# A graph layer on one core: row gathers listed behind the evictions of picked rows, each waiting for its eviction, where they were listed with the use of chunks

## The chip, the core and the metric

The kernel runs on one core of one Trainium2 chip. The metric is device time in microseconds (us), from the launch's start to its end. Times of the kernel before: 2096.8, 2087.51 and 2089.18 us, median 2089.18. A kernel's program keeps five queues of instructions: TensorE (PE, with its weight loads as PEld), VectorE (DVE), ScalarE (ACT), GpSimd (POOL) and SyncE (SP). Each queue runs in order, and semaphores tie the queues together.

## The reference

A graph layer with two kinds of edges, a residual connection and a layer norm. There are 12,500 nodes of 128 features and 400,000 edges, sorted by destination.

```python
Xs = X[src]
m_data = Xs @ W_data.T + b_data
m_ctrl = Xs @ W_control.T + b_control
msg = where(edge_types == 0, m_data, m_ctrl)
agg = segment_sum(msg, dst, num_segments=12500)
out = relu(agg + X @ W_self.T + b_self)
result = layernorm(X + out)
```

The kernel sums the source rows first and multiplies by the weights afterwards: for each node it needs the sum of the rows that come by edges of type 0, the sum of those of type 1, and how many there were of each (for the biases).

## The kernel before

**Chunks and groups.** The edges are cut into 3125 chunks of 128. 125 chunks make a group, 25 groups in all. A group has five windows of 5 "p" chunks and 20 "e" chunks; in odd groups the fifth window is 25 "p" chunks. That makes 865 p chunks, and 113 windows of e chunks, one after the other: the main loop's 113 steps (`for w in range(pairs)`, near the end of `short_path`).

**x in three parts.** Ahead of the loop, x is split into three bf16 parts whose sum is the f32 value. They stay in SBUF (`x3`) and are also written to DRAM as rows of 384 bf16 numbers (`rows3`).

**p chunks are gathered.** `fetch` (L721) takes a buffer `msg` from a pool of HOLD = 18 and lets GpSimd fetch 128 rows of `rows3` by an indirect DMA (L727). AHEAD = 14 of them are issued ahead of the loop. After that, `chunk` (L741) calls `fetch` once as it uses a chunk, so that the gather listed with chunk n is that of chunk n + 14. It can start once its buffer is free, which is when the matmuls of the chunk 18 before its own are done. Using a chunk takes three matmuls with a 0/1 matrix of destinations (`add_rows`, L677) and one that counts (L753); they add up in a PSUM tile `sums`, which VectorE adds to an accumulator (L715) when the window is done.

**e chunks are picked.** The rows of an e window are put into 98 blocks of 32 slots by the block of x that they come from. For each block TensorE multiplies a 0/1 matrix (`pick`) with that block of x in SBUF (L782), so that the wanted rows land in PSUM (`got`), four blocks in 128 rows. ScalarE evicts them to bf16 as `emsg`, two such sets at a time (L793, "the eviction of picked rows", 12 a step). TensorE then counts (L804) and adds them up (L677) as it does p chunks. Edges that don't fit in 32 slots, up to 64 a step, are fetched by one more indirect DMA of GpSimd into a tile `last` (`spare_rows`, L761); its index comes from VectorE (`idx`, L519). The other half of `last` is the two remaining blocks, evicted by L799.

**VectorE's part.** For each step VectorE works out which block and slot each edge gets, in a chain of bf16 operations: `O`, `prod`, `half`, `found`, `rm`, `rv` (L482 to L608). TensorE puts `rv` in place (`rk`, L620), ScalarE copies it (`cell`), and two DMAs of SyncE spread it over all partitions as the next steps' `pick` (L630, L632).

**What sets the order.** The kernel lists its work by fractions of a step: `evenly` gives units a place between 0 and 1, and `merged` (L142) sorts several streams by place and traces them in that order. The p chunks are spread evenly over all steps (`chunks`), at place `at` = LAG + (n + 0.5) (pairs - LAG) / total for the n-th. A step of `picked` (L766) is six units; unit t holds two evictions (`rows`, L787), and `spare_rows` is called in unit 2. A framework makes the engines' queues and the semaphores from the traced order; the changed program leaves the order on TensorE, VectorE, ScalarE and SyncE as it is. Each gather also waits for the landing of the one eight before it.

Of the kernel before, what the change touches and what calls it, by code (L numbers as in the profile page):

```python
# [9 lines left out]
BF = mybir.dt.bfloat16  # L10
# [7 lines left out]
P = 128  # L18
D = 128
# [4 lines left out]
NG = NC // GC  # L24
GN = P * GC * N // E
PB = 5
# [3 lines left out]
NE = 5  # L30
# [13 lines left out]
NCELL = 4 * NQ  # L44
OVF = 64
TOP = 7
SB = 1
HOLD = 18
AHEAD = 14
ACC_ROWS = 99 * P  # L50
# [97 lines left out]
def evenly(units, a=0.0, b=1.0):  # L148
    return [(a + (b - a) * (k + 0.5) / len(units), u) for k, u in enumerate(units)]


def short_path(ctx, tc, const, ident, eps, wT, brow, bad, x, src, dst, etype, ws, bs, out):
    nc = tc.nc
# [19 lines left out]
    def of_p(g, i):  # L173

        return PL if g % 2 and i == NE - 1 else PB
# [46 lines left out]
    for kind, i, c, _ in windows(0):  # L222
        if kind == "p":
            n = PL if i == NE - 1 else PB
            nc.sync.dma_start(
                out=near_i[i * PB:i * PB + n, :],
                in_=dst.rearrange("(o g e) -> o g e", o=1, g=NG)[:, :, c * P].to_broadcast([n, NG]),
# [6 lines left out]
    rows3 = dram.tile([N, 3 * D], BF, name="rows3")  # L234
# [181 lines left out]
    codes = {}  # L416
# [61 lines left out]
    def select(sel, col, code2):  # L478

        rows, n, width = sel.shape  # L480
        shape = [rows, n, width // 2, 2]
        nc.vector.tensor_tensor(  # L482
            sel.rearrange("p n (w t) -> p n w t", t=2),
            col[:rows].rearrange("p (o w t) -> p o w t", o=1, t=2).to_broadcast(shape),
            code2.rearrange("p n (o t) -> p n o t", o=1).to_broadcast(shape),
            op=OP.is_equal,
        )
        return sel
# [180 lines left out]
    def sums():  # L669
        return ps2.tile([P, 512], FP, name="sums")  # L670

    def cells_of(ps, width, k):
        return ps[:, k * 2 * width:(k + 1) * 2 * width]

    def add_rows(out, msg, sel, start, stop):
        for j in range(3):
            nc.tensor.matmul(  # L677
                out, msg[:, j * D:(j + 1) * D], sel, start=(start and j == 0), stop=stop, skip_group_check=True
            )
# [28 lines left out]
    def accumulate(g, i, ps, wide, width):  # L708

        begin_acc(g)  # L710
        parts_in[g] = parts_in.get(g, 0) + 1
        with tc.issue_after(added[-2].ins) if len(added) > 1 else ExitStack():
            at = nc.vector.value_load(raw["place"][0:1, g, i:i + 1], min_val=0, max_val=R - WMAX)
        win = acc[g][:, :, bass.ds(at, width)]
        added.append(nc.vector.tensor_add(win, win, ps[:, :4 * wide].rearrange("p (a w) -> p a w", w=wide)[:, :, :width]))  # L715


    to_fetch = [(g, i, c) for g in range(NG) for i in range(NE) for c in range(0, of_p(g, i), SB)]
    fetched = []

    def fetch():  # L721
        if to_fetch:
            g, i, c = to_fetch.pop(0)
            msg = mp.tile([P, SB, 3 * D], BF, name="msg")
            for k in range(min(SB, of_p(g, i) - c)):
                at = i * PB + c + k
                nc.gpsimd.indirect_dma_start(  # L727
                    out=msg[:, k, :], out_offset=None, in_=rows3[:, :],
                    in_offset=bass.IndirectOffsetOnAxis(ap=codes["p", g][0][:, at:at + 1], axis=0),
                )  # L730
            fetched.append(msg)

    def gathered(g, i):
        n = of_p(g, i)
        s = {}

        def choose():
            sel = sp.tile([P, PL, 2 * PW], BF, name="psel")[:, :n]
            s["sel"] = select(sel, near_col, codes["p", g][1][:, i * PB:i * PB + n])

        def chunk(c):  # L741
            if c % SB == 0:
                fetch()
                s["msg"] = fetched.pop(0)
            if c == 0:
                s["ps"] = sums()
                choose()
            sel = s["sel"][:, c].rearrange("p (t w) -> p t w", t=2)
            rows, cnt = (
                cells_of(s["ps"], AW, k).rearrange("p (t w) -> p t w", t=2)[:, :, DPC * c:DPC * c + PW] for k in range(2)  # L750
            )
            add_rows(rows, s["msg"][:, c % SB, :], sel, c == 0, c == n - 1)
            nc.tensor.matmul(cnt, one_col, sel, start=False, stop=(c == n - 1), skip_group_check=True)  # L753
            if c == n - 1:
                accumulate(g, 2 * i, s["ps"], AW, PW + DPC * (n - 1))

        return evenly([lambda c=c: chunk(c) for c in range(n)])

    def spare_rows(w):
        msg = slots[w]["last"] = two.tile([P, 3 * D], BF, name="last")  # L760
        nc.gpsimd.indirect_dma_start(  # L761
            out=msg[:OVF, :], out_offset=None, in_=rows3[:, :],
            in_offset=bass.IndirectOffsetOnAxis(ap=slots[w]["idx"], axis=0),
        )

    def picked(w, tiled, ending, fin_used, before):  # L766

        g, i = each_e[w]  # L770
        s = {"sel": {}, "msg": {}}
        per, pair = 4, 2

        def choose(q0, n=8):

            sel = select(sp.tile([P, 9, 2 * EW], BF, name="esel")[:, :n], code_col, slots[w]["code"][:, q0:q0 + n])
            for k in range(n):
                s["sel"][q0 + k] = sel[:, k]

        def pick(ps, q, a0=0):  # L780
            for a in range(a0, 4):
                nc.tensor.matmul(  # L782
                    ps[CAP * a:CAP * (a + 1), :], slots[w]["pick"][:, a * NQ + q, :],
                    x3[:, 4 * q + a - a0].rearrange("p j d -> p (j d)"), start=True, stop=True, skip_group_check=True,
                )

        def rows(q):  # L787
            ps = psg.tile([P, pair, 512], FP, name="got")
            msg = two.tile([P, pair, 3 * D], BF, name="emsg", bufs=5)
            for k in range(pair):  # L790
                pick(ps[:, k, :3 * D], q + k)
                s["msg"][q + k] = msg[:, k, :]
            nc.scalar.copy(msg, ps[:, :, :3 * D])  # L793

        def last_rows():
            q = NQ - 1
            ps = psg.tile([P, pair, 512], FP, name="got")[:, 0] if fin_used else ps1.tile([P, 512], FP, name="fin")
            pick(ps[:, :3 * D], q, 2)
            nc.scalar.copy(s["msg"][q][OVF:, :], ps[OVF:, :3 * D])  # L799

        def count(q):
            if q == 0:
                s["ps"] = sums()
            nc.tensor.matmul(  # L804
                cells_of(s["ps"], EW, 1)[CAP * (q % 4):CAP * (q % 4 + 1), :], one_col[:, :CAP], s["sel"][q],
                start=(q < 4), stop=(q + 4 >= NQ), skip_group_check=True,
            )

        def add(q0, q1):
            for q in range(q0, q1):  # L810
                add_rows(cells_of(s["ps"], EW, 0), s["msg"].pop(q), s["sel"][q], False, q == NQ - 1)

        def unit(t):

            for q in range(t * per, (t + 1) * per, pair):
                rows(q)
            if t == 1 and before:
                before()
            if t in (0, 1):
                choose(8 * t)  # L820
            if t == 0:
                ending()
            if t == 2:
                if w > 0:
                    spare_rows(w)
                s["msg"][NQ - 1] = slots[w]["last"]
            if t == 3:
                choose(16, 9)
            if t > 0:
                for q in range((t - 1) * per, t * per if t < turns - 1 else NQ):  # L830
                    count(q)
            if t == turns - 1:
                last_rows()
            if t > 0:
                add((t - 1) * per, t * per)
            for u in tiled.get(t, []):
                u()

        def end():

            add((turns - 1) * per, NQ)
            for u in tiled.get(turns, []):
                u()
            accumulate(g, 2 * i + 1, s["ps"], EW, EW)

        turns = (NQ - 1) // per
        return evenly([lambda t=t: unit(t) for t in range(turns)]), end


# [111 lines left out]
    mp = ctx.enter_context(tc.tile_pool(name="msg", bufs=HOLD))  # L961
# [9 lines left out]
    load(1, "p")  # L971
    for u in prep_p(0):
        u()
    for _ in range(AHEAD):
        fetch()


    chunks, closed, rest = {}, {}, []
# [1 line left out]
    n = 0  # L980
    for p in range(NG * NE):
        for _, u in gathered(*divmod(p, NE)):
            at = LAG + (n + 0.5) * (pairs - LAG) / total
            chunks.setdefault(int(at), []).append((at % 1, u))
            n += 1
        closed.setdefault(int(at), []).append(p)

    def ending():
        pass

    for w in range(pairs):
        g, i = each_e[w]
# [197 lines left out]
```

## Time and profile before

| what | us |
|---|---|
| median of the timed runs | 2089.18 |
| the profiled execution's own time | 2084.42 |
| its span, from first to last instruction | 2082.7 |
| TensorE busy between 110 and 2060 us | 1792.47 of 1950 |
| GpSimd's gathers busy, L727 | 1153.9, in 865 of 1334 ns on average |
| the same gathers, shortest, median, longest | 0.940, 1.058, 4.247 |
| one eviction L793, median | 0.798 |

The page's lines by groups give a line of the kernel, its engine and operation, what it writes and reads, the count, the busy time and the mean length of one, and after the last bar the time that its engine stood idle ahead of it and what ended that. "issue" is time in which an engine waited for nothing that the profile shows. The trace's first 110 us are the start-up (loads, the split of x, the first picks and gathers). The mean granted clock of TensorE is 0.986.

### The profile page before, as it was taken

The numbers are of one execution on the slowest core, as the hardware profiler recorded it, in microseconds if no ns is written. First come the engines' busy times: TensorE is split into PE (matmuls) and PEld (weight loads), VectorE is DVE, ScalarE is ACT, GpSimd is POOL, SyncE is SP. The second block draws the span as 40 slices with busy tenths as digits, with TensorE's granted clock in tenths as the row PEclk, the third lists the DMA queues.
The fourth block names the chain that finished last, engine by engine and source line by source line (L and its number), as shares of the span: only waits on it lengthen the run. The fifth ranks groups of instructions, "written<-read, shape, count | busy, mean of one in ns | idle before, by whom it ended". The sixth has DMA issues, their size and how long they took to land.

```text
span 2082.7 us, 75459 instructions
## 1 busy us (share of the span) xinstructions
PE 1828.3 (88%) x30869; PEld 1369.9 (66%) x30869; DVE 1718.1 (82%) x4707; ACT 1304.3 (63%) x2464; POOL 1296.7 (62%) x996
## 2 busy tenths in 40 slices
PE   0489889999999998899998999999999999999996
PEld 0367666676666776676666666766776676776675
DVE  7689788988887888888888888878888888888873
ACT  3466666666665666666566666656666666766665
POOL 0446567667667667567666566676676676665660
PEclk9999999999999999999999999999999999999998
DMA  7534343443443443433433434434434434434331
GB/s 213 185 107 134 107 136 102 139 136 98 135 136 97 135 131 102 133 121 112 126 105 118 130 101 134 133 101 134 133 97 132 136 99 132 134 107 132 122 98 33
DMA packets 186535, 254.92 MB, mean 122 GB/s; under 512 B 85369, under 2 KB 152995, under 8 KB 183108
## 3 DMA queue, kind: packets, MB, share of 16 engines
q1 hardware_dynamic: 128418, 152.97, 22.7%
q0 software_dynamic: 45136, 90.65, 15.5%
q10 hardware_dynamic: 12626, 6.40, 1.1%
q8 instruction: 243, 3.98, 0.8%
q14 instruction: 112, 0.92, 0.1%
HBM read 231.89 MB, written 18.04 MB: 120 GB/s over the span
## 4 chain that ended last, share of the span: by engine, by line
PE 56%; DVE 30%; ACT 5%; issue 4%; DMA 2%; another core or an unknown queue 1%; DVEq 1%; SPq 0%; ACTq 0%
PE sums L677 24%; PE got L782 18%; ACT emsg L793 4%; DVE esel L482 4%; PE rk L620 3%; DVE pick L662 3%; DVE prod L570 3%; DVE rv L608 3%; PE sums L804 2%; DVE found L579 2%; DVE prod L548 2%; DVE ahead L566 2%; PE rk L556 2%; PE rk L508 1%; DVE half L575 1%
## 5 line engine op out<-in xcount | busy, mean ns | idle before, releaser
L727 POOL DMA_INDIRECT msg<-rows,pidx x865 | 1153.9, 1334 | 619.9 <-PE sums L677 251.9
L793 ACT CAST emsg<-got 128x768 bf16<-128x768 f32 x1356 | 1035.6, 802 | 494.2 <-PE got L782 371.4
L677 PE MATMUL sums<-esel,emsg 128*128 128x176 bf16 x8136 | 755.5, 241 | 11.4 <-issue 10.8
L782 PE MATMUL got<-x,pick 128*32 128x384 bf16 x10896 | 664.7, 332 | 91.8 <-ACT emsg L793 60.8
L677 PEld LDWEIGHTS <-emsg 128*128 128x128 bf16 x8136 | 598.1, 98 | 169.0 <-issue 152.5
L782 PEld LDWEIGHTS <-pick 128*32 128x32 bf16 x11074 | 260.8, 95 | 255.3 <-issue 156.0
L482 DVE TENSOR_TENSOR esel<-code_col,code 128x1408 bf16<-128x1408 bf16 x339 | 308.9, 911 | 29.0 <-PE sums L677 13.6
L715 DVE TENSOR_TENSOR acc<-acc,sums 128x352 f32 (+2 forms) x238 | 102.0, 429 | 169.2 <-PE sums L677 79.7
L761 POOL DMA_INDIRECT last<-rows,idx x113 | 138.7, 1227 | 132.8 <-DMA bias<-b_parts 71.3
L677 PE MATMUL sums<-psel,msg 128*128 128x48 bf16 x2595 | 186.0, 184 | 12.2 <-DVE acc L715 7.8
L804 PE MATMUL sums<-esel,one_col 128*32 128x176 bf16 x2825 | 183.5, 242 | 9.0 <-issue 8.4
L677 PEld LDWEIGHTS <-msg 128*128 128x128 bf16 x2595 | 149.1, 97 | 21.0 <-issue 18.1
L620 PE MATMUL rk<-rv,O 128*128 128x64 bf16 x2260 | 90.5, 195 | 68.0 <-DVE rv L608 63.8
L662 DVE TENSOR_SCALAR pick<-pick,lane_f 128x1600 bf16<-128x1600 bf16 x226 | 142.8, 637 | 6.8 <-DMA pick<-there 4.2
L482 DVE TENSOR_TENSOR O<-cell_col,blk 128x2000 bf16<-128x2000 bf16 x113 | 134.7, 1192 | 15.1 <-PE fin L782 6.3
L753 PE MATMUL sums<-psel,one_col 128*128 128x48 bf16 x865 | 145.3, 183 | 0.2 <-issue 0.2
L620 PEld LDWEIGHTS <-O 128*128 128x128 bf16 x2260 | 83.2, 100 | 93.9 <-issue 92.9
L570 DVE TENSOR_TENSOR prod<-O,ahead 128x2000 bf16<-128x2000 bf16 x113 | 134.4, 1190 | 0.0
L804 PEld LDWEIGHTS <-one_col 128*32 128x32 bf16 x2825 | 86.6, 96 | 45.8 <-issue 16.7
L566 DVE TENSOR_REDUCE ahead<-rk 128x100 bf16<-128x500 f32 x113 | 76.2, 675 | 48.6 <-PE rk L498 21.3
L753 PEld LDWEIGHTS <-one_col 128*128 128x128 bf16 x865 | 82.7, 96 | 1.2 <-issue 1.1
L579 DVE TENSOR_REDUCE found<-half 128x20 f32<-128x520 bf16 x113 | 77.4, 685 | 0.0
(173 smaller groups left out, 2026.6 us busy)
## 6 DMA issues: line engine op xcount, KB each, us to landing
pick<-there SPq DMA_DIRECT2D x113, 800.0 KB
acc<-acc_start SPq DMA_DIRECT2D x23, 1280.0 KB
msg<-rows,pidx POOLq DMA_INDIRECT x865
rows<-x SPq DMA_DIRECT2D x6, 1344.0 KB
xs<-in_x_dram SPq DMA_DIRECT2D x99, 62.5 KB
out_dram<-h SPq DMA_DIRECT2D x99, 62.5 KB
xt<-in_x_dram ACTq DMA_DIRECT2D x6, 896.0 KB
there<-cell SPq DMA_DIRECT2D x113, 6.2 KB
```

The source lines that it names most:

```text
L482: nc.vector.tensor_tensor(sel.rearrange("p n (w t) -> p n w t", t=2), col[:rows].rearrange("p (o w t) -> p o w t", o=1, t=2).to_broadcast( ...
L570: nc.vector.tensor_tensor(prod, s["O"], ahead.rearrange("p (o j) -> p o j", o=1).to_broadcast([P, EC, NCELL]), op=OP.mult)
L579: nc.vector.tensor_reduce(found, half[:, :, :26], AX.X, OP.add)
L620: nc.tensor.matmul(s["rk"][:m, :2 * CAP], s["held"][:, c * NCELL:c * NCELL + m], s["rv"][:, c].rearrange("p v r -> p (v r)"), start=(c == ...
L662: nc.vector.tensor_scalar(t, t, lane_f, None, op0=OP.is_equal)
L677: nc.tensor.matmul(out, msg[:, j * D:(j + 1) * D], sel, start=(start and j == 0), stop=stop, skip_group_check=True)
L727: nc.gpsimd.indirect_dma_start(out=msg[:, k, :], out_offset=None, in_=rows3[:, :], in_offset=bass.IndirectOffsetOnAxis(ap=codes["p", g][0] ...
L753: nc.tensor.matmul(cnt, one_col, sel, start=False, stop=(c == n - 1), skip_group_check=True)
L761: nc.gpsimd.indirect_dma_start(out=msg[:OVF, :], out_offset=None, in_=rows3[:, :], in_offset=bass.IndirectOffsetOnAxis(ap=slots[w]["idx"], ...
L782: nc.tensor.matmul(ps[CAP * a:CAP * (a + 1), :], slots[w]["pick"][:, a * NQ + q, :], x3[:, 4 * q + a - a0].rearrange("p j d -> p (j d)"), ...
L793: nc.scalar.copy(msg, ps[:, :, :3 * D])
L804: nc.tensor.matmul(cells_of(s["ps"], EW, 1)[CAP * (q % 4):CAP * (q % 4 + 1), :], one_col[:, :CAP], s["sel"][q], start=(q < 4), stop=(q + 4 ...
```

## The change

Gathers are no longer listed by `chunk`. A list `due` holds, for each gather, the place at which the chunk 14 before its own is used, and 0 for the first 14, which are still issued ahead of the loop. After each eviction of picked rows, `paced` is called with the place of that eviction. If a gather of spare rows is on the list `spare`, it is issued; else, if the next gather's due place is reached, that one is; else none. So at most one gather stands behind each eviction. `tc.add_manual_dep(..., Sync, DATA)` makes the gather wait on a semaphore until that eviction is done. The gather of spare rows moves from unit 2 to the first eviction of unit 1. The constant SB, which was 1, is gone, and with it the loop over SB.

```diff
-    to_fetch = [(g, i, c) for g in range(NG) for i in range(NE) for c in range(0, of_p(g, i), SB)]
-    fetched = []
+    to_fetch = [(g, i, c) for g in range(NG) for i in range(NE) for c in range(of_p(g, i))]
+    fetched, due, spare = [], [], []
...
+    def paced(now, gate):
+
+        if spare:
+            gather = spare.pop()()
+        elif to_fetch and due[len(due) - len(to_fetch)] <= now:
+            gather = fetch()
+        else:
+            return
+        tc.add_manual_dep(
+            gather.ins, gate.ins.name,
+            mybir.DependencyInfo(mybir.DependencyClass.Sync, mybir.DependencyReason.DATA), reason="paced",
+        )
...
         def chunk(c):
-            if c % SB == 0:
-                fetch()
-                s["msg"] = fetched.pop(0)
+            s["msg"] = fetched.pop(0)
...
-            nc.scalar.copy(msg, ps[:, :, :3 * D])
+            paced(w + (q + 1) / (turns * per), nc.scalar.copy(msg, ps[:, :, :3 * D]))
...
+            if t == 1 and w > 0:
+                spare.append(lambda: spare_rows(w))
...
             if t == 2:
-                if w > 0:
-                    spare_rows(w)
+                assert not spare
...
+            due.append(at)
             n += 1
...
+    due[:] = [0.0] * AHEAD + due[:-AHEAD]
+    for _ in range(AHEAD):
+        fetch()
```

More of the change, by code (lines that the diff above doesn't have):

```diff
@@ L46 @@
 TOP = 7
-SB = 1
 HOLD = 18
@@ L715, in accumulate @@
         added.append(nc.vector.tensor_add(win, win, ps[:, :4 * wide].rearrange("p (a w) -> p a w", w=wide)[:, :, :width]))
-    to_fetch = [(g, i, c) for g in range(NG) for i in range(NE) for c in range(0, of_p(g, i), SB)]
-    fetched = []
+    to_fetch = [(g, i, c) for g in range(NG) for i in range(NE) for c in range(of_p(g, i))]
+    fetched, due, spare = [], [], []
     def fetch():
[L722 to L731, printed above, removed]
+        g, i, c = to_fetch.pop(0)
+        msg = mp.tile([P, 3 * D], BF, name="msg")
+        at = i * PB + c
+        fetched.append(msg)
+        return nc.gpsimd.indirect_dma_start(
+            out=msg, out_offset=None, in_=rows3[:, :],
+            in_offset=bass.IndirectOffsetOnAxis(ap=codes["p", g][0][:, at:at + 1], axis=0),
+        )
[9 more added lines that the diff above has]
+            mybir.DependencyInfo(mybir.DependencyClass.Sync, mybir.DependencyReason.DATA), reason="paced",
+        )
     def gathered(g, i):
@@ L751, in chunk @@
             )
-            add_rows(rows, s["msg"][:, c % SB, :], sel, c == 0, c == n - 1)
+            add_rows(rows, s["msg"], sel, c == 0, c == n - 1)
             nc.tensor.matmul(cnt, one_col, sel, start=False, stop=(c == n - 1), skip_group_check=True)
@@ L760, in spare_rows @@
         msg = slots[w]["last"] = two.tile([P, 3 * D], BF, name="last")
-        nc.gpsimd.indirect_dma_start(
+        return nc.gpsimd.indirect_dma_start(
             out=msg[:OVF, :], out_offset=None, in_=rows3[:, :],
@@ L973, in short_path @@
         u()
-    for _ in range(AHEAD):
-        fetch()
     chunks, closed, rest = {}, {}, []
```

## The prediction

> **What bounds the kernel now.** I read the page's busy times, its chain, the waits, then TensorE's and GpSimd's timelines where TensorE stands still.
>
> ```profile
> PE 1828.3 (88%) x30869; PEld 1369.9 (66%) x30869; DVE 1718.1 (82%) x4707; ACT 1304.3 (63%) x2464; POOL 1296.7 (62%) x996
> ...
> PE 56%; DVE 30%; ACT 5%; issue 4%; DMA 2%; another core or an unknown queue 1%; DVEq 1%; SPq 0%; ACTq 0%
> ...
> L727 POOL DMA_INDIRECT msg<-rows,pidx x865 | 1153.9, 1334 | 619.9 <-PE sums L677 251.9
> ```
>
> TensorE bounds it, with VectorE close behind. GpSimd's gathers (L727) are nowhere on the chain, and the view of waits has no row in which TensorE waits for a gather: each is issued some 17 chunks ahead. So the data's lateness costs nothing now. What the gathers do to others while they are issued is another matter:
>
> ```profile
> 71.70:87.10 15.40, 13.77 (x178) 8.72 (x177) 14.95 (x43) 12.64 (x19) 9.47 (x5) 1.00 0.51 147
> 87.10:107.10 20.00, 5.19 (x60) 2.95 (x59) 0.00 (x0) 1.54 (x5) 13.24 (x14) 0.68 0.36 117
> 107.10:122.50 15.40, 14.70 (x228) 10.44 (x227) 14.50 (x41) 11.11 (x24) 2.61 (x2) 0.86 0.28 100
> ```
>
> The columns of the view by windows are window, length, then busy time (count) of PE, PEld, DVE, ACT and POOL, clock, DMA share, GB/s. From 87.1 to 107.1 us GpSimd issues 14 gathers without a pause; TensorE works 5.19 of 20 us, VectorE not at all. Before and behind it TensorE is 89 and 95% busy. The same in small, first POOL's timeline (start, length, instruction, idle time before it and its releaser):
>
> ```profile
> 1037.76 0.95 POOL L727 DMA_INDIRECT msg<-rows,pidx  x1 [0.31 <-PE got L782]
> 1039.01 0.95 POOL L727 DMA_INDIRECT msg<-rows,pidx  x1 [0.30 <-issue]
> 1040.26 0.95 POOL L727 DMA_INDIRECT msg<-rows,pidx  x1 [0.30 <-issue]
> 1041.51 0.94 POOL L727 DMA_INDIRECT msg<-rows,pidx  x1 [0.30 <-issue]
> ```
>
> and PE's:
>
> ```profile
> 1040.53 0.36 PE L782 MATMUL got<-x,pick 128*32 128x384 bf16 x4 [0.20 <-issue]
> 1041.24 0.35 PE L782 MATMUL got<-x,pick 128*32 128x384 bf16 x2 [0.34 <-issue]
> 1041.96 0.50 PE L782 MATMUL got<-x,pick 128*32 128x384 bf16 x5 [0.37 <-issue]
> 1043.41 0.52 PE L782 MATMUL got<-x,pick 128*32 128x384 bf16 x3 [0.95 <-issue]
> ```
>
> Four gathers 1.25 us apart; from the third on, matmuls that take 0.83 us for sixteen elsewhere come in handfuls, and wait for nothing the profile names ("issue"). I counted this over the whole trace between 110 and 2060 us. Wherever three gathers start within 3.0 us (94 times, a "close triple"), I took the 2.5 us from the third start, 82 stretches once merged, and asked for them as windows:
>
> ```profile
> sum 221.13, PE 160.24 PEld 109.07 DVE 175.55 ACT 110.67 POOL 153.32; mean PE 1.95 PEld 1.33 DVE 2.14 ACT 1.35 POOL 1.87
> ```
>
> against the whole stretch:
>
> ```profile
> 110.00:2060.00 1950.00, 1792.47 (x30482) 1346.19 (x30478) 1636.86 (x4476) 1254.63 (x2392) 1269.06 (x959) 0.99 0.39 119
> ```
>
> TensorE idles 221.1 - 160.2 = 60.9 us (28%) there, and 157.5 - 60.9 = 96.6 us of the other 1728.9 (5.6%). The excess is 60.9 - 0.056 x 221.1 = **48.5 us**; the triples closer than 2.6 us alone (68.8 us of stretches, 39.4 busy) carry 24.7 of it by the same working. Seven stretches of 3.4 us at clock 0.50 begin within 4 us of a close triple (at 220.7, 558.6, 1012.6, 1043.3, 1104.8, 1142.3, 1569.0). At half clock each loses about 1.6 us: 11 us.
>
> **The change, part by part.** On TensorE, VectorE, ScalarE and SyncE both built programs have the same instructions in the same order. Only GpSimd's queue differs: the same 865 + 113 gathers, with "last" (L761) standing before 4 or 5 gathers that were ahead of it, in 105 of 113 steps.
>
> *Later start.* 847 gathers waited for the third matmul of the chunk 18 before theirs (their buffer); now 852 wait for an eviction listed near the chunk 14 before. A chunk takes 1950/865 = 2.25 us, so a gather starts about 9 us later, 14 x 2.25 = 31 us ahead of its use. How long it takes to land is bounded by the queue: gather n+8 waits for n, and these ran 1.25 us apart, so under 10 us. 21 us of cover remain: cost 0. The cover is gone only if GpSimd falls nine gathers behind; then each costs up to its 1.33 us.
>
> *The wait.* It replaces a wait, and the queue's in-order rest is gathers alone, with the same cover. TensorE signals less: third matmul to next is 25 ns with a signal and 25 ns between chunks without. 0.
>
> *"last".* It waits for its index (L519) and an eviction. Laid over this trace, that eviction ends 0.7 us (median) behind the index, so the index holds nobody, and "last" starts within 1.3 us of where it did, in nine steps of ten. Its use stood 9.9 us off at the least. 0.
>
> *Start-up.* 18 gathers run on from 79.91 us; only the first 14 (AHEAD) stay ungated. Four at 1.25 us go out of the stall: **-5.0**. Ends: 0 (something else ends it) and -18.3 (the chain's two unknown pieces there, 10.85 + 7.48).
>
> *Close triples.* At most one gather behind each eviction does not forbid them. I laid the new gates, the ends of the evictions named in the changed program, against the old ones, the releases. Three gates within 2.6 us: 157 against 261; within 3.0 us: 265 against 309, so between 2.6 and 3.0 us there are more, 108 against 48. I take 40% off the first group: 0.4 x 24.7 = 9.9, and 0 for the second, since most of its stretches cost little (TensorE idles 553 ns at 2.75 to 3.0, 179 ns from 3.0). What TensorE regains reaches the end as far as the chain is its own: PE, ACT and issue, 65%. **-6.4**. Ends: -38 (79%, the 74 of 94 triples with fewer than three evictions ended in them, all regained) and +14 (60 more of the second group at 23.8/64 = 0.37 us, by 65%).
>
> *Clock.* 40% of 11 us, by 65%: **-2.9**. Ends 0 and -8.7 (79%).
>
> Sum: 5.0 + 6.4 + 2.9 = 14.3 us off the profiled execution's 2084.4: 2070. The three timed runs' median is 4.8 us above that execution, so I forecast **2075 us**, 0.7% less.
>
> **The Trainium skill.** The page "SBUF — State Buffer" (section "Who interferes with whom") says that a DMA never contends with a compute engine and that PE and ACT never wait on anyone. By that rule the three terms are 0 and the profiled execution stays at 2084.4. The rows 87.10:107.10 and 1040.53 speak against it, but may have another reason.
>
> **The rivals.**
> *No change, 2089.* The stalls and the strings of gathers have a common cause, or the same number of triples forms again. For it: 61 of the 94 triples stand behind a gather that took over 1.7 us, beside bf16 work of VectorE; the backlog then runs off through gates long passed, old or new. VectorE's heavy phase also keeps TensorE waiting. Against it: the start-up, where VectorE did nothing.
> *Slower, 2104.* The gates themselves come in threes. Evictions end in twos, 0.70 us apart (1.50 us "x2" in ScalarE's rows), twelve a step for nine gathers, so a pair and the next eviction often all carry one. Place: TensorE in every step; price +14 us (above), with nothing won elsewhere: 2084.4 + 14.4 + 4.8. It decides if three starts 2.6 to 3.0 us apart cost TensorE as much as this trace's mean of that group.
> *More, 2024.* Every end on the side of a gain at once, -18.3 - 38 - 8.7 = -65 off 2089. It needs nearly all triples gone and the start-up stall too; only the 20 triples in which three evictions ended speak against the first, and the 14 ungated gathers against the second.
>
> **How the numbers follow.** Forecast 0.48 (2060 to 2083), no change 0.28 (2081 to 2097), slower 0.16, more 0.08. The range runs from halfway between "more" and the forecast's lower edge to a little past "slower", 2042 to 2106; about 2 in 10 lies outside, with cases not named here. Half a per cent (10 us) is about what a measurement here can tell from no change. Faster by more, under 2079: most of the forecast and all of "more", 0.48. Within: 0.35. Slower by more, over 2100: 0.17.
>
> **What would show it.** The stall at start-up ends near 102 us instead of 107. Close triples fall well under 94 and the close ones under 2.6 us by about 40%; TensorE's idle time between 110 us and the end falls from 157 toward 145; fewer than seven half-clock stretches; GpSimd waits for ACT (eviction) instead of PE. It is wrong if triples fall and TensorE's idle time stays, or if the string at start-up shrinks and the stall does not.

## The result, and the profile after

The changed kernel took **2192.73 us** (median of 4 runs, 2188.6 to 2197.08), the kernel before 2092.99 beside it: a ratio of 1.0477, 95% interval 1.0435 to 1.0518. It is 4.8% slower, where 2075 (2042 to 2106) was forecast. The profiled execution took 2189.8 us, its span is 2188.1, the mean granted clock 0.977.

One thing has to be told ahead of everything else. The runs were made in seven sittings, each on one chip with the kernel before in it. In four (this result's is one) the kernel before took 2087 to 2104 us, in three 1941 to 1944, and the change costs 5% in the first kind (two sittings) and nothing in the second (the one of the three in which the changed kernel ran). The seven are called **late** and **prompt** sittings below, for a reason that the traces give.

First the page of the changed kernel: busy times, the chain, the group of gathers.

```profile
PE 1874.3 (86%) x30869; PEld 1385.2 (63%) x30869; DVE 1723.4 (79%) x4707; ACT 1299.1 (59%) x2464; POOL 1288.3 (59%) x996
...
PE 58%; DVE 20%; ACT 8%; issue 6%; DMA 3%; another core or an unknown queue 3%; POOL 0%; DVEq 0%; SPq 0%; ACTq 0%; POOLq 0%
...
L725 POOL DMA_INDIRECT msg<-rows,pidx x865 | 1137.9, 1316 | 664.5 <-ACT emsg L801 411.5
```

As forecast, GpSimd now waits for ScalarE's evictions (L801, before L793) instead of TensorE. But VectorE's share of the chain fell from 30% to 20%, while ScalarE, "issue" and "unknown queue" grew from 5 + 4 + 1 to 8 + 6 + 3%. The view of waits (engine and line, what it waited for, us in total, times, longest) says who:

```profile
PE got L790 <- ACT emsg L801: 81.1, 184, 1.6
ACT emsg L801 <- remote: 78.4, 38, 4.0
...
PE got L790 <- issue: 43.6, 129, 1.1
```

and the same three of the kernel before:

```profile
PE got L782 <- ACT emsg L793: 60.8, 105, 7.7
...
ACT emsg L793 <- remote: 27.7, 12, 7.6
...
PE got L782 <- issue: 24.9, 78, 1.0
```

"remote" stands where a wait ends on a signal that the trace can't ascribe. There is no other core here: ScalarE stood idle ahead of an eviction although nothing it needs was still at work. One such place, from 1145 us; POOL's, ACT's and PE's timelines (start, length, instruction, idle time before it and its releaser):

```profile
1145.39 0.94 POOL L725 DMA_INDIRECT msg<-rows,pidx  x1 [0.30 <-issue]
1146.64 0.90 POOL L769 DMA_INDIRECT last<-rows,idx  x1 [0.30 <-issue]
1147.85 1.15 POOL L725 DMA_INDIRECT msg<-rows,pidx  x1 [0.31 <-issue]
1150.86 0.95 POOL L725 DMA_INDIRECT msg<-rows,pidx  x1 [1.87 <-ACT emsg L801]
```

```profile
1146.19 0.48 ACT L807 CAST last<-fin 64x384 bf16<-64x384 f32 x1
1149.80 1.50 ACT L801 CAST emsg<-got 128x768 bf16<-128x768 f32 x2 [3.13 <-remote]
```

```profile
1146.69 0.83 PE L790 MATMUL got<-x,pick 128*32 128x384 bf16 x16
...
1148.14 0.54 PE L676 MATMUL sums<-esel,emsg 128*128 128x176 bf16 x5 [0.28 <-issue]
...
1150.65 0.51 PE L790 MATMUL got<-x,pick 128*32 128x384 bf16 x8 [0.59 <-ACT emsg L801]
```

Both evictions' picks end at 1146.69 + 0.83 = 1147.52; ScalarE has been free since 1146.67; yet the first eviction starts at 1149.80, **over 2.2 us late**. TensorE works on in handfuls, then waits 0.59 us for that eviction, and the next gather waits for it too (1.87).

I took this for every eviction from 110 us to 25 us before the end: from the later of the end of ScalarE's previous instruction and the end of the last pick that ended ahead of its start, to its start, counted where over 0.15 us. The moment it counts from is the eviction's release. That pick can be one for the next eviction, so a late start is a lower bound. The **late starts** of evictions sum to 142 us in the kernel before and 244 in the changed one. That is 102 us more, and the span is 105.4 longer. (Counted from each eviction's own eighth pick, the sums are 230 and 340; two expectations below name 106 and 181 us, an earlier count that the record does not define.) The traces show the late start. That it is TensorE's signal that comes late, as it is called below, and not something else that holds ScalarE up, is a reading of them. In both kernels the lateness falls on evictions released 0 to 1.2 us behind the end of a gather (0.18 us each on average before, 0.33 after); from 1.4 us on the mean is under 0.06. Close triples (three gathers that start within 3.0 us, the third between 110 and 2060 us) rose from 94 to 161, those within 2.6 us from 30 to 58; half-clock stretches from 7 to 17. The windows, as for the kernel before, start-up first, then the whole main part:

```profile
87.10:107.10 20.00, 7.66 (x77) 4.35 (x75) 6.49 (x21) 4.87 (x13) 14.20 (x14) 0.63 0.57 185
...
110.00:2060.00 1950.00, 1737.69 (x28740) 1284.40 (x28733) 1566.40 (x4284) 1178.35 (x2261) 1200.33 (x920) 0.98 0.38 115
```

TensorE idles 212 of these 1950 us, where it was 157.

### The profile page after: what moved, and what is told of

Its sections match the earlier page's. It is cut to its first block, busy times and chain, and to the rows that moved or that the text cites. A ratio compares the mean times of both kernels' runs of the same rounds, so it can differ in the third digit from the quotient of the medians.

```text
span 2188.1 us, 75470 instructions
## 1 busy us (share of the span) xinstructions
PE 1874.3 (86%) x30869; PEld 1385.2 (63%) x30869; DVE 1723.4 (79%) x4707; ACT 1299.1 (59%) x2464; POOL 1288.3 (59%) x996
## 3 DMA queue, kind: packets, MB, share of 16 engines
q0 software_dynamic: 45136, 90.65, 14.8%
## 4 chain that ended last, share of the span: by engine, by line
PE 58%; DVE 20%; ACT 8%; issue 6%; DMA 3%; another core or an unknown queue 3%; POOL 0%; DVEq 0%; SPq 0%; ACTq 0%; POOLq 0%
PE sums L676 23%; PE got L790 22%; ACT emsg L801 6%; PE rk L619 3%; DVE esel L481 2%; PE sums L812 2%; DVE pick L661 2%; PE fin L911 2%; DVE prod L569 2%; DVE rv L607 2%; PE rk L555 1%; PE rk L507 1%; DVE found L578 1%; DVE prod L547 1%
## 5 line engine op out<-in xcount | busy, mean ns | idle before, releaser
L725 POOL DMA_INDIRECT msg<-rows,pidx x865 | 1137.9, 1316 | 664.5 <-ACT emsg L801 411.5
L801 ACT CAST emsg<-got 128x768 bf16<-128x768 f32 x1356 | 1033.6, 804 | 574.2 <-PE got L790 345.3
L676 PE MATMUL sums<-esel,emsg 128*128 128x176 bf16 x8136 | 775.2, 243 | 31.2 <-issue 29.8
L790 PE MATMUL got<-x,pick 128*32 128x384 bf16 x10896 | 682.2, 334 | 129.9 <-ACT emsg L801 81.1
L676 PEld LDWEIGHTS <-emsg 128*128 128x128 bf16 x8136 | 604.4, 99 | 204.6 <-issue 188.9
L790 PEld LDWEIGHTS <-pick 128*32 128x32 bf16 x11074 | 266.4, 95 | 298.2 <-issue 200.5
L769 POOL DMA_INDIRECT last<-rows,idx x113 | 146.3, 1294 | 203.6 <-ACT emsg L801 122.2
L627 ACT CAST cell<-rk 128x64 bf16<-128x64 f32 x113 | 24.2, 214 | 90.4 <-PE fin L790 34.0
```

What stands on the lines that cost most here:

```text
L676: nc.tensor.matmul(out, msg[:, j * D:(j + 1) * D], sel, start=(start and j == 0), stop=stop, skip_group_check=True)
L725: return nc.gpsimd.indirect_dma_start(out=msg, out_offset=None, in_=rows3[:, :], in_offset=bass.IndirectOffsetOnAxis(ap=codes["p", g][0][: ...
L769: return nc.gpsimd.indirect_dma_start(out=msg[:OVF, :], out_offset=None, in_=rows3[:, :], in_offset=bass.IndirectOffsetOnAxis(ap=slots[w][ ...
L790: nc.tensor.matmul(ps[CAP * a:CAP * (a + 1), :], slots[w]["pick"][:, a * NQ + q, :], x3[:, 4 * q + a - a0].rearrange("p j d -> p (j d)"), ...
L801: paced(w + (q + 1) / (turns * per), nc.scalar.copy(msg, ps[:, :, :3 * D]))
```

## The experiments

Two theories went into the first sitting: **succession** (gathers close behind one another stall TensorE, and the change made more of them) and **lock-step** (the tie to evictions costs by itself). A third, of **place** (late signals belong to the chip, or to where it ran, and not to the program), came with its results. A kernel's ratio is to the kernel before of the same sitting.

### Prompt sitting, before 1943.7: two in flight, last ungated, lists of three

Two in flight, on the kernel before:

```diff
+                if len(gathers) > 2:
+                    tc.add_manual_dep(gathers[-1].ins, gathers[-3].ins.name, ...Sync, ...DATA...)
```

> The kernel before, with one wait more: each gather of a p chunk also waits until the gather two ahead of it has landed, so three can no longer run off 1.25 us apart. Two theories. Succession: gathers in close succession stall TensorE and bring on half clock, and the change made more of them. Lock-step: it is the wait for ScalarE that costs, by tying GpSimd to ScalarE and both to TensorE. Succession expects close triples (three starts within 3.0 us, 94 in the kernel before) nearly gone, and with them most of the 48.5 us of excess idle time of TensorE and the 11 us of half clock: 2040 to 2070 us, against 2093 before. Lock-step expects no gain, 2093 us, or a loss if the landings come late enough to hold GpSimd up.

2256.69 us, 1.1624 (1.1577 to 1.167): neither theory. Gathers of p chunks now wait 245.4 us for the landing of earlier ones. The gathers of spare rows stand where they did in GpSimd's queue (109 of 113), among gathers that wait, and TensorE now stands for them:

```profile
PE sums L677 <- DMA last<-rows,idx: 238.2, 66, 9.8
```

Nor did the limit do what it was for: 117 close triples remained. It tells nothing of either theory.

> The changed kernel, its waits for evictions kept, with the same wait for the landing of the gather two ahead. Succession expects the loss gone and more: 2040 to 2080 us, with close triples well under 94 (161 in the changed kernel). Lock-step expects the loss to stay, about 2190 us, since every gather still waits for ScalarE.

The same on the changed kernel: 2238.98, 1.1533 (1.1509 to 1.1557), for the same reason (257.2 us of waits for landings, 230.8 of TensorE for spare rows).

Next, on the changed kernel, the gather of spare rows is called in unit 2 again and loses its wait:

```diff
-            if t == 1 and w > 0:
-                spare.append(lambda: spare_rows(w))
...
             if t == 2:
-                assert not spare
+                if w > 0:
+                    spare_rows(w)
```

> The changed kernel, but the gather of spare rows is issued in unit 2 as before and neither waits for an eviction nor takes an eviction's place. The other 851 gathers keep their waits. In the changed program the place it takes puts four or five gathers behind consecutive evictions. Succession expects fewer close triples than 161, some 120 to 145, and 2130 to 2180 us. Lock-step expects 2185 to 2195. A third theory, that it was the gather of spare rows with its own wait that cost the time, expects 2093.

1941.3, 0.9984 (0.9967 to 1.0001): no slower than before, but with 350 close triples, not fewer. In GpSimd's queue all 113 gathers of spare rows stand where they do in the changed kernel. What this takes back is their wait and the place that each took at an eviction.

Gathers in lists of up to three, on the kernel before:

```diff
-SB = 1
-HOLD = 18
-AHEAD = 14
+SB = 3
+HOLD = 6
+AHEAD = 5
```

> The kernel before with SB = 3 instead of 1, HOLD = 6 and AHEAD = 5: gathers are listed up to three at a time (3 + 2 in a window of five chunks), into one buffer that is freed as a whole; no wait for ScalarE. Succession expects close triples to rise well over 161, since nearly each list of three is one, and the time with them: 2180 to 2350 us. Lock-step expects about 2093.

1939.07, 0.9976 (0.9959 to 0.9993), with 372 close triples. Succession had expected 2180 to 2350. **As a law of the kernel alone it fell here**: close gathers cost nothing in this sitting. And the kernel before, at 1943.7, was 149 us faster than beside the result. The sum of late starts in these four traces is 0, 0, 0 and 0.2 us.

### Late sitting, before 2090.1: changed and before again, last gated alone

> The changed kernel, unaltered, on the chip that runs this job. In the first four runs the kernel before took 1943.7 us, where it took 2093 beside the changed kernel, and the two runs with as many or more close triples (350 and 372) showed TensorE idle for only 0.06 of the 2.5 us after a triple, where it was 0.28 and 0.32 before. A theory of place: the stall behind close gathers belongs to the chip (or to where it ran), not to the program; on a chip without it the changed kernel takes what the kernel before does, within 0.5%: 1935 to 1950 if that is 1943. If it was the gather of spare rows with its own wait (which the run without it can't rule out), the changed kernel is slower than before by 3 to 5% on this chip too: 2000 to 2040.

2189.35, 1.0505 (1.0437 to 1.0573): the result again, late starts 219 us.

> The kernel before, unaltered, for its trace on this chip. By place: if it takes about 1943 us, the waits of TensorE for nothing (issue), 48.5 us in the profile first shown, are gone, the start-up string of gathers no longer stops TensorE from 87 to 107 us, and the half-clock stretches behind triples are gone. If they are there and the time is about 1943 all the same, the stalls were never what cost the time.

One execution, 2084.51: late starts 145 us, 101 close triples, as in the first profile.

Then, on the kernel before, `rows` calls the gather of spare rows behind unit 1's first eviction, with its wait:

```diff
+            gate = nc.scalar.copy(msg, ps[:, :, :3 * D])
+            if q == per and w > 0:
+                tc.add_manual_dep(spare_rows(w).ins, gate.ins.name, ...Sync, ...DATA...)
```

> The kernel before, with one part of the change alone: the gather of spare rows is listed behind the first eviction of unit 1 and waits for it; the other gathers stay listed with the use of chunks and wait for their buffer. By place: within 0.5% of the kernel before on this chip. If this gather with its wait is what costs the time: 3 to 5% slower.

2097.2, 1.0037 (1.0004 to 1.007). The wait of this gather alone is worth 0.4% of the 5. Its place in GpSimd's queue stayed that of the kernel before, within one gather.

### Prompt sitting, before 1941.52: the changed kernel, and three more

> The changed kernel, unaltered, once more. So far the kernel before took 2093 and 2090 us in two jobs, with the changed kernel 5% slower in both, and 1944 us in a third, in which the changed kernel wasn't run. The two traces of that job without a limit on flights show no eviction that starts over 0.11 us after TensorE's last matmul for it and ScalarE's previous work are both done (99 of 100), where before and after have a sum of 106 and 181 us of such lateness, nearly all within 1.4 us of a gather's end. Theory of place: late signals exist on some chips only. Where the kernel before takes about 1944, the changed kernel takes 1935 to 1955; where it takes about 2090, 2185 to 2200.

1939.65, **0.9989** (0.9971 to 1.0008). The same program, instruction by instruction, that is 5% slower in a late sitting costs nothing here. Its page:

```profile
PE 1746.2 (90%) x30869; PEld 1350.3 (70%) x30869; DVE 1715.6 (89%) x4707; ACT 1302.4 (67%) x2464; POOL 1347.8 (70%) x996
...
DVE 53%; PE 31%; DMA 9%; ACT 3%; issue 3%; DVEq 1%; SPq 0%; POOL 0%; ACTq 0%
```

VectorE has the largest share of the chain; the unknown queue is off the chain, and no wait of an eviction is put down to "remote". Now a string of three gathers (POOL), the evictions in it (ACT) and their picks (PE):

```profile
1046.33 0.94 POOL L725 DMA_INDIRECT msg<-rows,pidx  x1 [0.30 <-DVE acc L714]
1047.58 0.95 POOL L725 DMA_INDIRECT msg<-rows,pidx  x1 [0.30 <-ACT cnt L889]
1048.83 1.37 POOL L769 DMA_INDIRECT last<-rows,idx  x1 [0.30 <-ACT emsg L801]
```

```profile
1049.20 1.50 ACT L801 CAST emsg<-got 128x768 bf16<-128x768 f32 x2 [0.51 <-PE got L790]
```

```profile
1048.58 0.83 PE L790 MATMUL got<-x,pick 128*32 128x384 bf16 x16
```

Gathers as close as those of 1145.39, but the first of the two evictions starts at 1049.20, as the first eight of the sixteen picks end, where it came 2.2 us behind them all. And this is the sum of TensorE's windows behind all 363 close triples of this trace: it idles 42.9 of 668.4 us, 6.4%, against 31.5% in the changed kernel of the result.

```profile
sum 668.40, PE 625.54 PEld 486.29 DVE 622.72 ACT 471.16 POOL 544.91; mean PE 4.04 PEld 3.14 DVE 4.02 ACT 3.04 POOL 3.52
```

> The changed kernel with the gather of spare rows ungated, as before in unit 2, once more, for a chip with late signals. Succession (the strings of four and five consecutive gates that this gather's place makes are what costs): 2110 to 2160 where the changed kernel takes 2190. Lock-step (each gather that starts as an eviction ends lets its own late signals fall on the next evictions): 2175 to 2195. Where the kernel before takes 1944: 1935 to 1950 by both.

1940.22, 1.0001 (0.9978 to 1.0024).

> Before with gathers listed in threes (SB = 3), once more, for a chip with late signals. Succession: far more close triples than 161, so slower than the changed kernel, 2200 to 2350 us. Lock-step: no gate at an eviction, so about as before, 2080 to 2110. Where the kernel before takes 1944: 1935 to 1945 by both.

1943.17, 1.0001 (0.9979 to 1.0022).

```diff
-                    out=msg[:, k, :], out_offset=None, in_=rows3[:, :],
+                    out=msg[:, k, :D], out_offset=None, in_=rows3.rearrange("n (t d) -> (n t) d", t=3)[:, :],
...
-                out, msg[:, j * D:(j + 1) * D], sel, ...
+                out, msg[:, j * step * D:(j * step + 1) * D], sel, ...
```

(`step` is 0 for p chunks.)

> The kernel before, in which a gather of a p chunk brings 128 numbers a row instead of 384, from other places of the same table, and TensorE uses them for all three parts: two of the three parts are left out, and the rows are wrong ones; the matmuls are as many and as long, the gathers as many with as many rows. If it is the bytes under way that make signals late, their sum falls by half or more, and on a chip with late signals the time falls to 2000 to 2050 us. If it is the issue or the number of rows, it stays at 2075 to 2105. Where the kernel before takes 1944: 1930 to 1945.

1932.43, 0.9942 (0.9918 to 0.9965).

### Late sitting, before 2104.04: what makes more lateness

> Before with gathers listed in threes (SB = 3). On a chip where the kernel before takes about 2090 us and signals come late behind gathers, succession (closeness of gathers is the cost) expects many more close triples than 161 and 2200 to 2350 us; lock-step (a gather that starts as an eviction ends makes the next evictions' signals late) expects about as before, 2080 to 2110. Where the kernel before takes 1942 it tells nothing: 1935 to 1945 again.

2263.58, **1.0734** (1.0694 to 1.0775). Close triples 199, late starts 216 us, half-clock stretches 35 (six of them 6.8 us long, the others 3.4). No gather waits for an eviction here. Succession's number, in a sitting where signals are late; lock-step expected none of it. Evictions wait 132.0 us on "remote", 78.4 in the changed kernel. The windows behind its close triples, 34% idle:

```profile
sum 439.52, PE 288.54 PEld 186.88 DVE 274.77 ACT 162.27 POOL 270.40; mean PE 1.91 PEld 1.24 DVE 1.82 ACT 1.07 POOL 1.79
```

> The changed kernel with the gather of spare rows ungated. On a chip where the kernel before takes about 2090, succession expects 2110 to 2160 (the strings of four and five are gone), lock-step 2175 to 2195. Where it takes 1942: 1935 to 1945.

2212.62, 1.0516 (1.0479 to 1.0553); late starts 238 us, 126 close triples. The strings of four and five gates that the gather of spare rows makes are not the cause: without them the loss is the same. Here lock-step was nearer.

> Before with gathers of p chunks that bring 128 numbers a row instead of 384, used for all three parts (two of the three parts and the right rows are left out). On a chip where the kernel before takes about 2090: 2000 to 2050 if the bytes under way make signals late, 2075 to 2105 if the issue or the count of rows does. Where it takes 1942: 1930 to 1940, as measured.

2102.43, 0.9994 (0.9963 to 1.0025); late starts 155 us. The page shows 33.96 MB and 31,296 packets in GpSimd's DMA queue, where the kernel before has 90.65 MB and 45,136, and nothing changes. So it isn't the amount of data under way that makes signals late. What is left is the issue of a gather, the number of its rows, or something else in it that no run varied.

### Prompt, before 1941.25, then late, before 2086.59: a distance between gathers

```diff
+        for _ in range(3):
+            with tc.issue_after(pad[-1].ins):
+                pad.append(nc.gpsimd.iota(pad[0], pattern=[[1, 40]], base=0, channel_multiplier=0))
```

> The kernel before with three small iotas of GpSimd (128x40, into a tile that nobody reads) issued behind every gather, in that order, so that two gathers can't start closer than about 1.25 + 3 x 0.15 = 1.7 us (a 128x48 iota took 0.157 us). The work of the other engines and its order are unchanged. Closeness as the cost, on a chip where the kernel before takes about 2090: close triples (under 3.0 us) nearly gone, and 2020 to 2075 us. If closeness only goes along with something else, or GpSimd falls behind with (1.33 + 0.30 + 0.45) us for each of 978 gathers, near its whole time: no gain or slower, 2085 to 2200. Where the kernel before takes 1942: 1940 to 2050, since 978 x 2.1 us is more than that.

> The changed kernel with the same three iotas behind every gather. Closeness, on a chip where the kernel before takes about 2090: the changed kernel's loss (2190) goes too, 2020 to 2100 us, within 1.5% of the kernel before with iotas. If the tie to evictions costs by itself, it stays 3% or more behind that one.

> The kernel before with lists of three (2264 us, 1.073 of the kernel before, on such a chip) and the same three iotas behind every gather. Closeness: its loss goes, 2020 to 2110 us. If the lists cost by the buffer that is freed as a whole, it stays at 2200 or more.

2483.8, 2488.39 and 2304.73 (1.2788, 1.2793, 1.189), far over the 1940 to 2050 that was expected of the first in such a sitting. With the iotas gathers that follow at once start mostly 2.13 us apart (1.71 at the least). No close triple is left, but GpSimd falls behind: in the first, TensorE waits 407.2 us for gathers of spare rows. That, and a prompt sitting, make the three empty for the question.

> The changed kernel with one iota of 128x40 behind every gather instead of three: 0.18 us and, as the kernel with three showed, 0.23 us more of idle time ahead of the next gather, so gathers start no closer than 1.65 us and three starts span 3.3 us or more. GpSimd has 868 us of idle time ahead of gathers in the changed kernel, 293 of it the 0.30 us that stand ahead of each; 978 x 0.41 = 401 us fit in. On a chip with late signals (before about 2090) closeness expects the sum of late starts of evictions well under 181 us, no close triples, and 2060 to 2150 us, where the changed kernel takes 2190; a cost of the tie to evictions by itself expects 2180 or more. On a chip without (before 1942): 1940 to 2000, as GpSimd has less time to spare there.

2190.12, 1.0475 (1.0412 to 1.0539), in a late sitting. POOL's timeline shows why this is no dose either:

```profile
1009.10 0.19 POOL L726 IOTA pad<- 128x40 int32 x1
1009.44 1.04 POOL L722 DMA_INDIRECT msg<-rows,pidx  x1 [0.16 <-issue]
```

One iota fits into the 0.30 us that stand ahead of a gather anyway. Gathers still start 1.29 us apart, 150 close triples remain, late starts sum to 217 us. The same closeness gave the same time; closeness was not taken away.

### All late sittings beside the prompt ones

| kernel | span, late | late starts, us | close triples | span, prompt |
|---|---|---|---|---|
| before (first profile, repeated) | 2082.7, 2082.8 | 142, 145 | 94, 101 | no trace; medians 1942.0, 1939.8, 1939.5 |
| third of the bytes | 2091.6 | 155 | 91 | 1935.7 |
| last gated alone | 2097.2 | 160 | 116 | not run |
| changed (result, repeated) | 2188.1, 2184.2 | 244, 219 | 161, 152 | 1935.6 |
| changed, last ungated | 2201.5 | 238 | 126 | 1933.1, 1932.5 |
| changed, one iota | 2187.3 | 217 | 150 | not run |
| lists of three | 2266.0 | 216 | 199 | 1937.4, 1942.6 |

In the prompt sittings the sum is under 0.5 us in every trace. What a kernel loses from prompt to late is near its sum of late starts: 143 us against 142 (before, from 1940), 156 against 155 (a third of the bytes), 253 against 244 and 249 against 219 (changed), 269 against 238 (last ungated). That is a likeness and no account of the time: lists of three lose 326 with a sum of 216, half-clock stretches are in no sum, and from each eviction's own picks the sums are larger (230 before, 340 changed).

The traces allow a finer sorting than by triples. Call gathers a string where each starts under 1.5 us behind the one before, and put each eviction to the gather that started last ahead of its release, if that one ended at most 1.4 us before. The mean late start, in us, then grows with the length of the string, with gates at evictions and without:

| kernel, late sittings | alone | two | three | four or more |
|---|---|---|---|---|
| before | 0.02 | 0.21 | 0.39 | 1.06 (8 evictions) |
| changed | 0.04 | 0.33 | 0.41 | 0.76 |
| changed, last ungated | 0.06 | 0.28 | 0.54 | 0.83 |
| lists of three | 0.02 | 0.25 | 0.33 | 0.91 |

Farther behind a gather it is 0.00, and so it is in strings of every length in the prompt trace of the changed kernel. Strings of two or more have 455 evictions in the kernel before and 553 in the changed one. So a gather alone costs next to nothing, a pair costs already, and pairs are in no count of triples. It is a sorting and no experiment, since a late eviction also holds gathers back. Pairs cost more in the changed kernel than before (0.33 against 0.21), so their number alone does not give the whole loss.

## Why the prediction was wrong, step by step

**What bounds it.** Right that TensorE did in that execution, and that a part of its waits for nothing lies behind close gathers. Wrong to take that for a property of the program. The kernel before took 149 us less in a prompt sitting. It left no trace there, but the changed kernel and the kernel before with a third of the bytes did: they have no late starts, and VectorE has 53 and 55% of the chain, TensorE 31 and 28. One profile can't tell that.

**Later start of gathers, the wait itself, "last".** 0, 0 and 0 were right as far as the data's cover goes: the two late traces of the changed kernel have no wait of TensorE for a gather, the prompt one has a single one (11.9 us, for "last"), and in that sitting all three together cost nothing (0.9989). Where signals are late, "last" with its wait alone costs 0.4%, and its release gives nothing back. Whether the wait of the other gathers costs by itself there stays open.

**Start-up, -5.0.** Not shown. The forecast sign came: TensorE works 7.66 of the 20 us from 87.1, where it worked 5.19, and ScalarE's evictions are back at 101.5 instead of 107. But the unaltered kernel before, run again, has it too: evictions are back at 102.4, and these two rows of its windows give 8.52 of 20 us.

```profile
87.10:102.10 15.00, 5.58 (x59) 3.55 (x57) 3.80 (x17) 2.02 (x6) 11.80 (x11) 0.70 0.71 228
102.10:107.10 5.00, 2.94 (x18) 0.75 (x19) 0.42 (x1) 2.55 (x6) 3.80 (x4) 0.50 0.29 79
```

So this stall differs between executions of one kernel by about as much as the change was to win.

**Close triples, -6.4.** This step failed, in sign and size. I laid the new gates over the old trace's evictions, found fewer close ones within 2.6 us (157 against 261) and took 40% off. On the chip they rose from 30 to 58, where the working would give 18. The step also put the 64 triples between 2.6 and 3.0 us at nothing because they "cost little", though its own 553 ns of 2.5 us are 22% idle, against 5.6% elsewhere; 39 more of these came. And it counted no pairs, which the table above shows to cost.

Why the laying-over failed is argued, not shown. A gate laid over an old trace holds still; a real one moves with the lateness that the gathers cause. A late eviction holds its gather back, and the next gates may open with little between them. Of the strings within 2.6 us, those that begin within 1.5 us behind the end of a late eviction, with no gather over 1.7 us at their start or among the two ahead, are 11 of 48 in the changed kernel and 15 of 56 in its repeat, against 2 of 25 and 3 of 31 in the kernel before. That fits a loop from lateness to closeness to lateness. But in the changed kernel gathers wait for evictions anyway, with "last" ungated it is only 7 of 50 at the same loss, and no run took closeness away in a late sitting.

**Clock, -2.9.** Wrong in sign with the step above: 7 stretches became 17.

**The rivals.** "The gates themselves come in threes" had the direction and the place. Its price, +14 us, was the mean stall of the old trace times 60 more triples. Of the 67 triples that came, 54 lie within 2.75 us. In the changed kernel TensorE idles 1.07 us in the 2.5 us behind the third start of those within 2.6, and 0.81 up to 2.75. And the lateness reached evictions elsewhere: most of what the sum grew lies outside the surroundings (1.5 us ahead to 2.5 us behind) of triples within 2.6 us. "No change" came true in the prompt sitting alone, at 1940 us.

**What would show it.** Neither sign of a wrong mechanism came as it was put: triples did not fall while idle time stayed. They rose, and TensorE's idle time with them (157 to 212 us). That bears out the link between the two in a late sitting, and goes against the step that was to lower them.

**The rule of the Trainium skill.** In the prompt sittings the trace agrees with "SBUF — State Buffer", section "Who interferes with whom" (a DMA never contends with a compute engine; PE and ACT wait on nobody): 363 close triples, no eviction over 0.11 us late. In the late ones evictions of the changed kernel start up to 3.6 us late behind gathers, so the rule, taken as widely as I took it, doesn't hold there. The section speaks of ports to SBUF; whether these have a part in the lateness, no run here shows.

**What stays open.** What differs between sittings, whether the chip or something that is set up anew each time. The record gives chip number 0 to a prompt sitting and, nine minutes later, to a late one; if that number means the same chip, then it isn't the chip. What in a gather delays a signal: not the amount of its data; issue and number of rows were not told apart. How much of the 5% is closeness and how much the tie to evictions: lists of three, without a tie, show that closeness suffices for a loss; "last" ungated, with fewer triples (126) and the same loss, shows that their number doesn't say all. And the place of "last" in GpSimd's queue, four or five gathers further forward in all runs of the changed kernel, was taken back by none; of the changed kernel's 85 strings of three gathers or more, 25 have a "last" in them and 7 begin with one.

## What to carry to other kernels

Before a stall is priced from a profile, ask whether it is the program's: a stall whose waits end on nothing that the trace names ("issue", "remote") may be absent the next time, and then everything built on it is worth nothing; run the kernel before again elsewhere, with a trace. A gate that hangs one engine's transfers on the end of another engine's work passes each delay of that work on to the transfers, so the old trace's releases, laid under the new gates, give the order and not the spacing. A measure that covers an effect as a whole (here the lateness of each eviction against what it really waits for) says more than the windows in which it was first noticed, but it must say from which moment it counts: here that makes 142 or 230 us of the same trace.

## What the runs showed of the hardware that was not expected

- Behind a gather of GpSimd, an eviction of ScalarE can start late, with its picks done and ScalarE free: by a mean of 0.18 to 0.33 us where it is released in the first 1.2 us behind the gather's end, by 3.6 us at most in the changed kernel, and 5.0 in any. The mean grows with the number of gathers in a string (0.02, 0.21 and 0.39 us for one, two and three in the kernel before). In prompt sittings, with the same programs among them, it is never over 0.4 us in 11 traces.
- Around a triple within 2.6 us in the kernel before, several engines work less. From 2 to 1 us ahead of the third start ScalarE's busy share falls from 0.52 to 0.33 and VectorE's from 0.80 to 0.64; TensorE's falls from 0.90 half a us ahead of it to 0.44 one us behind it (means of half a us).
- Traces of late sittings hold fewer records of ScalarE's signals: 1781 of 2102 in the changed kernel, 2067 of 2102 for the same program in a prompt one. Whether this has to do with the lateness was not tested.
- Three iotas behind a gather mostly cost GpSimd 0.88 us (2.13 us between starts instead of 1.25), one iota 0.04.
